# A graph network of four layers: output biases in one product, gate bias on VectorE, counting in bf16

## The chip, the cores and the metric

The kernel runs on one core of a Trainium2 chip. The metric is device time in microseconds (us) for one execution, as the median of several runs. Engines are called as in the profile: PE (TensorE; its weight loads are PEld), DVE (VectorE), ACT (ScalarE), POOL (GpSimd) and SP (SyncE, which here only issues transfers). A line of the kernel is written L2968, and a line number is always that of the kernel before.

## The reference

The input `x` has 3125 rows (nodes) of 256 numbers, and there are 50,000 edges. Four times a graph layer is added to `x`, and after each a feed-forward layer (FFN); each works on the normalised rows of `x`. The graph layers are a SAGE layer, a layer with 16 edge types (the relation layer), one attention layer, and a pair of attention layers. Two of the FFNs matter here. The one after the relation layer sends each row to one of eight experts, with a fixed capacity of rows for each:

```python
idx = jnp.argmax(probs, axis=-1)
one_hot = jax.nn.one_hot(idx, E, dtype=jnp.float32)
pos = (jnp.cumsum(one_hot, axis=0) * one_hot).sum(-1).astype(jnp.int32) - 1
kept = pos < C
```

The last one has a shared network and four experts, of which a row takes the best two, weighed by a softmax over their gates:

```python
h = jax.nn.relu(jnp.einsum('baf,efh->ebah', x, eW1) + eb1[:, None, None, :])
h = jax.nn.relu(jnp.einsum('ebah,ehg->ebag', h, eW2) + eb2[:, None, None, :])
o = jnp.einsum('ebag,ego->ebao', h, eW3) + eb3[:, None, None, :]
...
gates = jax.nn.softmax(x @ gW + gb, axis=-1)
...
return shared + gated
```

Here `shared` is a network of three layers whose last bias is `sb3`. Everything is f32.

## The kernel before

The rows stand in 25 tiles of 128 rows (the last has 53). The edges are sorted by destination and are worked through in 98 groups of four chunks of 128 edges. For each chunk POOL gathers the source rows from a table with an indirect transfer (L295). PE multiplies them with a matrix of zeros and ones, or of coefficients, into PSUM. DVE adds the result to the sums of the destination tiles: at L1423 in the attention layers, and at L2122 in the relation layer.

As soon as a destination tile has all its edges it is closed, and its share of the next step is put on a queue of generators, `self.queue`. `serve()` is called between edge groups and runs two to four steps of the front generators up to their next `yield`. So a row's routing, or a block of the last FFN, is woven into the edge work in small steps. The final order on each engine is then set by a scheduler that has its own estimate of each instruction. Each engine works its instructions in that order.

**The routing** (`switch_route`, from L2128) lies inside the relation layer, from about 1725 to 2225 us. `route(t)` normalises tile `t`, transposes it on PE (L2164), multiplies it with the gate weights (L2170), takes the softmax on DVE and ACT, and picks the best expert (`argmax`, L1666 to L1676), which gives `oh`, a 128x8 tile of zeros and ones. Two products on PE (L2186 and L2187) count the choices of the rows ahead of each row in the tile, and of the whole tile. The weights of these products are `self.tri` and `self.ones`, both 128x128. DVE adds up the counts and the place of each row (L2189 to L2205), and POOL later scatters the tile's rows into the experts' buffer (`post`, L2218). On PE the neighbours of these products are L2113, which multiplies gathered rows with spread coefficients (`terms_of`, made on DVE at L2098), and L2051, which closes a tile.

**The last FFN** (`expert_block`, from L2879) lies inside the second of the last two attention layers, from about 4400 us to the end. Its weights are loaded by `expert_weights` at about 3554 us. There are 13 blocks, one of a single tile and twelve of two. A block is normalised (L2890 to L2896) and transposed (L2904). PE makes the gates (L2915), with the gate bias as a product of one row of ones and the bias (L2916). ACT copies the gates out of PSUM (L2918). Then `expert_gates` turns them into weights on DVE and ACT (from L2859), while `layer` makes the shared and the experts' hidden layers on PE (L2923) and ACT (L2924). The gate weights are transposed on PE (L2953) and copied to `wT` by ACT (L2955). A product with `pick` spreads them (L2959) for a multiplication on DVE (L2962). For each tile of the block the output is one sum in PSUM:

```python
nc.tensor.matmul(ps[:, :D], h2[:, o], w["s3"], start=True, stop=False)                    # L2967
nc.tensor.matmul(ps[:, :D], self.ones[0:1, :], w["sb3"], start=False, stop=False)         # L2968
nc.tensor.matmul(ps[:, :D], wT[:, o], w["eb3"], start=False, stop=False)                  # L2969
...
    nc.tensor.matmul(ps[:, :D], f2[:, q, o], w["e3"][:, q, :], start=False, stop=(q == NE // 2 - 1))  # L2971
```

DVE adds it to `x` (L2974), and SP writes the tile out (L2975).

Around the last FFN, the attention layer has its own work. PE multiplies scaled rows with the edge matrices (L2514) and adds up which edges reach a row (L2398, in bf16, with the matrix `member` from a transfer). DVE and ACT scale the gathered rows `ga` (L2505 and L2510). The first two destination tiles have so many edges that they are done apart: their weights are made on DVE (L2617, L2658, L2665) and ACT (L2651, L2661) and multiplied on PE (L2669).

Of the kernel before, what the change touches and what calls it, by code (L numbers as in the profile page):

```python
# [30 lines left out]
F32 = mybir.dt.float32  # L31
I32 = mybir.dt.int32
BF16 = mybir.dt.bfloat16
F16 = mybir.dt.float16
AF = mybir.ActivationFunctionType
# [1066 lines left out]
class SortedNet(Net):  # L1102
# [1025 lines left out]
    def switch_route(self, pool):  # L2128
        nc, tc = self.nc, self.tc
        pre = "L1_ffn_"  # L2130
        NE = NE8
        wg = pool.tile([P, 2, NE], F32, name="wg")
        nc.sync.dma_start(out=wg, in_=self.ins[pre + "gate_w"].rearrange("(k p) e -> p k e", p=P))
        bg = self.load_spread(pool, pre + "gate_b", NE)
        rank = pool.tile([P, NE], F32, name="rank")
        nc.vector.tensor_scalar(rank, self.iota_row[:, :NE], -1.0, float(NE), op0=ALU.mult, op1=ALU.add)
        count = pool.tile([P, NT + 1, NE], F32, name="count")
        nc.vector.memset(count[:, 0, :], 0.0)
        tok = pool.tile([P, NT], F32, name="tok")
        nc.vector.tensor_scalar(  # L2140
            tok, self.iota_row[:, :NT], float(P), float(NE * SLOTS), op0=ALU.mult, op1=ALU.add
        )
        nc.vector.tensor_scalar(tok, tok, self.iota_col, None, op0=ALU.add)
        base = pool.tile([P, NE], F32, name="base")
        nc.vector.tensor_scalar(base, self.iota_row[:, :NE], float(SLOTS), None, op0=ALU.mult)
        self.sw_prb = self.keep.tile([P, NT], F32, name="sw_prb")
        self.sw_from = self.keep.tile([P, NT], I32, name="sw_from")

        def route(t):
            edge = self.edge  # L2150
            st = edge.tile([P, 6], F32, name="sw_st", bufs=2)
            mv = edge.tile([P, 2], F32, name="sw_mv", bufs=2)
            rs = edge.tile([P, 1], F32, name="sw_rs", bufs=2)
            nc.vector.bn_stats(out=st, in_=self.x[:, t, :])
            nc.vector.bn_aggr(out=mv, in_=st)
            nc.scalar.activation(rs, mv[:, 1:2], AF.Sqrt, bias=self.eps)
            yield
            nc.vector.reciprocal(rs, rs)
            row = edge.tile([P, D], F32, name="sw_row", bufs=6)
            nc.vector.tensor_scalar(row, self.x[:, t, :], mv[:, 0:1], rs, op0=ALU.subtract, op1=ALU.mult)  # L2160
            yield
            ps = self.bank("aux")
            for k in range(2):
                nc.tensor.transpose(ps[:, k * P : (k + 1) * P], row[:, k * P : (k + 1) * P], self.ident)  # L2164
            rT = edge.tile([P, 2, P], F32, name="sw_rT", bufs=2)
            nc.scalar.activation(rT, ps[:, : 2 * P].rearrange("p (k n) -> p k n", k=2), AF.Copy)
            yield
            ps = self.bank("aux")
            for k in range(2):
                nc.tensor.matmul(ps[:, :NE], rT[:, k, :], wg[:, k, :], start=(k == 0), stop=(k == 1))  # L2170
            g = edge.tile([P, 1, NE], F32, name="sw_g", bufs=2)
            g2 = g.rearrange("p o e -> p (o e)")
            m = edge.tile([P, 1], F32, name="sw_m", bufs=2)
            nc.vector.tensor_add(g2, ps[:, :NE], bg)
            nc.vector.tensor_reduce(m, g2, axis=AX.X, op=ALU.max)
            nc.vector.tensor_scalar(g2, g2, m, None, op0=ALU.subtract)
            nc.scalar.activation(g2, g2, AF.Exp)
            yield
            nc.vector.tensor_reduce(m, g2, axis=AX.X, op=ALU.add)
            nc.vector.reciprocal(m, m)  # L2180
            nc.vector.tensor_scalar(g2, g2, m, None, op0=ALU.mult)
            best, oh = self.argmax(edge, g, rank, 1, NE, "sw")
            oh = oh.rearrange("p o e -> p (o e)")
            yield
            ps = self.bank("aux")
            nc.tensor.matmul(ps[:, :NE], self.tri, oh, start=True, stop=True)  # L2186
            nc.tensor.matmul(ps[:, NE : 2 * NE], self.ones, oh, start=True, stop=True)  # L2187
            yield
            nc.vector.tensor_add(count[:, t + 1, :], count[:, t, :], ps[:, NE : 2 * NE])  # L2189
            place = edge.tile([P, 2, NE], F32, name="sw_place", bufs=2)  # L2190
            nc.vector.tensor_add(place[:, 0, :], ps[:, :NE], count[:, t, :])
            nc.vector.tensor_mul(place[:, 0, :], place[:, 0, :], oh)
            nc.vector.tensor_mul(place[:, 1, :], base, oh)
            spot = edge.tile([P, 4], F32, name="sw_spot", bufs=2)
            nc.vector.tensor_reduce(spot[:, 0:2], place, axis=AX.X, op=ALU.add)
            pos, eid, kept, to = (spot[:, i : i + 1] for i in range(4))
            nc.vector.tensor_scalar(kept, pos, float(CAP), None, op0=ALU.is_lt)
            nc.vector.tensor_mul(self.sw_prb[:, t : t + 1], best, kept)
            nc.vector.tensor_add(to, eid, pos)
            nc.vector.tensor_sub(to, to, tok[:, t : t + 1])  # L2200
            nc.vector.tensor_mul(to, to, kept)
            to_i = edge.tile([P, 1], I32, name="sw_to", bufs=6)
            nc.vector.tensor_add(to_i, to, tok[:, t : t + 1])
            nc.vector.tensor_scalar(pos, pos, float(CAP - 1), None, op0=ALU.min)
            nc.vector.scalar_tensor_tensor(  # L2205
                self.sw_from[:, t : t + 1], eid, CAP / SLOTS, pos, op0=ALU.mult, op1=ALU.add
            )
            self.posted.append((t, row, to_i))
            self.routes = t + 1

        return route
# [604 lines left out]
    def expert_weights(self, pool):  # L2816
# [5 lines left out]
        def load(name, shape, source, rows=None, **sizes):  # L2822
            w[name] = pool.tile(shape, F32, name="se_" + name)
            nc.sync.dma_start(out=w[name], in_=source.rearrange(rows, **sizes) if rows else source)
# [10 lines left out]
            nc.sync.dma_start(out=w["e2"][:, e, o : o + E2], in_=ins[pre + "eW2"][e])  # L2835
        load("e3", [P, NE // 2, D], ins[pre + "eW3"].rearrange("(q o) p d -> (o p) q d", o=2))
        load("gw", [P, 2, NE], ins[pre + "gW"], "(k p) e -> p k e", p=P)
        load("gb", [1, NE], ins[pre + "gb"], "(o d) -> o d", o=1)
        load("sb3", [1, D], ins[pre + "sb3"], "(o d) -> o d", o=1)
        load("eb3", [NE, D], ins[pre + "eb3"])  # L2840
        for name, n in (("sb1", 2), ("sb2", 1), ("eb1", NE), ("eb2", NE // 2)):
            a = ins[pre + name]
            rows = self.work.tile([n, P], F32, name="colrows", tag="colrows", bufs=1)
# [35 lines left out]
    def expert_block(self, w, ts):  # L2879
# [32 lines left out]
        for i in range(n):  # L2912
            o = pg[:, i * NE : (i + 1) * NE]
            for k in range(2):
                nc.tensor.matmul(o, xT[:, k, i * P : (i + 1) * P], w["gw"][:, k, :], start=(k == 0), stop=False)  # L2915
            nc.tensor.matmul(o, self.ones[0:1, :], w["gb"], start=False, stop=True)  # L2916
        g = pool.tile([P, n, NE], F32, name="se_g", tag=f"se_g{n}", bufs=1)
        nc.scalar.activation(g, pg[:, : n * NE].rearrange("p (t e) -> p t e", e=NE), AF.Copy)  # L2918

        def layer(out, weights, inputs, bias):  # L2920
            ps = self.bank("aux")
# [28 lines left out]
        yield  # L2950
        pt = self.bank("aux")
        for i in range(n):
            nc.tensor.transpose(pt[:NE, i * P : (i + 1) * P], g[:, i, :], self.ident)  # L2953
        wT = pool.tile([NE, most], F32, name="se_wT", bufs=1)[:, :N_]
        nc.scalar.activation(wT, pt[:NE, :N_], AF.Copy)  # L2955
        yield
        for q in range(NE // 2):
            ps = self.bank("aux")
            nc.tensor.matmul(  # L2959
                ps[:, :N_], w["pick"].rearrange("k e j -> k (e j)")[:, q * P : (q + 1) * P], wT, start=True, stop=True  # L2960
            )
            nc.vector.tensor_mul(f2[:, q, :], f2[:, q, :], ps[:, :N_])  # L2962
        yield
        for i, t in enumerate(ts):
            o = slice(i * P, (i + 1) * P)
            ps = self.bank("aux")
            nc.tensor.matmul(ps[:, :D], h2[:, o], w["s3"], start=True, stop=False)  # L2967
            nc.tensor.matmul(ps[:, :D], self.ones[0:1, :], w["sb3"], start=False, stop=False)  # L2968
            nc.tensor.matmul(ps[:, :D], wT[:, o], w["eb3"], start=False, stop=False)  # L2969
            for q in range(NE // 2):  # L2970
                nc.tensor.matmul(ps[:, :D], f2[:, q, o], w["e3"][:, q, :], start=False, stop=(q == NE // 2 - 1))  # L2971
            r = rows_of(t)
            xt = self.x[:r, t, :]
            nc.vector.tensor_add(xt, xt, ps[:r, :D])  # L2974
            nc.sync.dma_start(out=self.out[t * P : t * P + r, :], in_=xt)  # L2975
            yield
# [112 lines left out]
```

## Time and profile before

| | |
|---|---|
| median of 3 runs | 4983.29 us (4973.4 to 4994.1) |
| the profiled execution | 4999.19 us |
| its span in the profile | 4997.2 us |
| PE busy | 3314.8 us, 66% |
| DVE busy | 2510.3 us, 50% |
| POOL busy | 2194.3 us, 44% |
| ACT busy | 1126.5 us, 23% |

All durations in the text come from this one profiled execution. An f32 product shows as two records of PE and two weight loads, so L2968, with 25 tiles, has 50 records. "Granted clock" is the share of PE's full clock that the throttle let through in a stretch. In the views, what stands in brackets behind a row is how long the engine was idle before it and what ended that; "issue" is idle time that nothing in the profile explains.

### The profile page before, as it was taken

The page shows a single profiled execution, that of the slowest core. Times are in us where ns is not written, and L with a number is a line of the kernel's source. Part 1 is how long each engine was busy: PE and PEld are TensorE (multiplying, and loading weights), DVE is VectorE, ACT ScalarE, POOL GpSimd, SP SyncE. Part 2 cuts the span into 40 slices and gives each one's busy share as a digit, 9 for nine tenths or more (in the row PEclk, how much of TensorE's full clock was granted, in tenths as well). Part 3 has the DMA queues.
Part 4 walks back from the last instruction along what each step waited for, and adds up shares of the span by engine and source line. Part 5 has one row for each costly group of instructions (what it writes and reads, how often), then busy time and mean ns, then how long its engine had stood idle before and what let it go on. Part 6 is the DMA issues. An engine that isn't in the chain of part 4 may idle for free. (4 is left out here: it accounts for less than half of the span.)

```text
span 4997.2 us, 58241 instructions
## 1 busy us (share of the span) xinstructions
PE 3314.8 (66%) x14775; PEld 2550.4 (51%) x14775; DVE 2510.3 (50%) x8714; ACT 1126.5 (23%) x3308; POOL 2194.3 (44%) x2222
## 2 busy tenths in 40 slices
PE   3885565547985577879843565559626666278887
PEld 1554444436944566766532453449514544156665
DVE  4763253357742355651154665533536655366655
ACT  1100000012420011112221342114213522135433
POOL 3656466621046665510045556220356553554451
PEclk9997787757956777889955676669756777578878
DMA  4455366432253332223234555412445554444451
GB/s 125 128 158 145 114 181 168 112 125 76 70 174 92 90 88 81 78 69 97 66 99 122 139 150 149 140 69 72 116 128 152 158 158 129 124 125 126 135 145 53
DMA packets 423800, 590.33 MB, mean 118 GB/s; under 512 B 117955, under 2 KB 304374, under 8 KB 423076
## 3 DMA queue, kind: packets, MB, share of 16 engines
q0 software_dynamic: 106416, 287.01, 21.6%
q1 hardware_dynamic: 313838, 296.31, 19.3%
q10 hardware_dynamic: 3206, 3.20, 0.2%
q8 instruction: 125, 2.05, 0.2%
q14 instruction: 215, 1.76, 0.1%
HBM read 480.53 MB, written 105.71 MB: 117 GB/s over the span
## 5 line engine op out<-in xcount | busy, mean ns | idle before, releaser
L295 POOL DMA_INDIRECT ga<-gat_table,src_i x960 | 976.2, 1017 | 859.0 <-issue 348.9
L2514 PE MATMUL mm<-ga,oh 128*128 128x260 f32 x1920 | 685.8, 512 | 221.4 <-issue 98.7
L295 POOL DMA_INDIRECT ga<-sage_t,src_i x576 | 566.3, 983 | 369.3 <-issue 152.6
L2514 PEld LDWEIGHTS mm<-ga,oh 128*128 128x128 f32 x1920 | 461.3, 255 | 331.3 <-issue 124.6
L295 POOL DMA_INDIRECT ga<-rel_x,src_i x391 | 379.3, 970 | 249.9 <-issue 106.5
L2113 PE MATMUL mm<-terms_of,ga 128*128 128x128 f32 (+9 forms) x1564 | 306.0, 353 | 179.5 <-issue 73.3
L1447 PE MATMUL mm<-ga,oh 128*128 128x257 f32 x1152 | 327.4, 432 | 99.4 <-DVE acc L1423 36.7
L1423 DVE SCALAR_TENSOR_TENSOR acc<-mm,low,acc 128x260 f32 (+1 forms) x384 | 185.5, 483 | 375.6 <-PE mm L2514 114.2
L2113 PEld LDWEIGHTS mm<-terms_of,ga 128*128 128x128 f32 x1564 | 265.0, 242 | 212.4 <-issue 88.1
L1447 PEld LDWEIGHTS mm<-ga,oh 128*128 128x128 f32 x1152 | 240.3, 217 | 166.7 <-issue 41.1
L1934 POOL DMA_INDIRECT yt<-slot_y_d,from_i x100 | 99.2, 992 | 511.1 <-DVE terms_of L2098 225.4
L2505 DVE TENSOR_TENSOR ga<-ga,p 128x768 f32<-128x768 f32 x240 | 228.8, 955 | 74.9 <-issue 51.4
L2510 ACT ACTIVATE ga<-ga,p 128x64 f32<-128x64 f32 x960 | 259.6, 334 | 4.3 <-issue 3.6
L2122 DVE TENSOR_TENSOR terms<-terms,mm 128x256 f32 (+9 forms) x296 | 135.5, 458 | 236.7 <-remote 80.4
L1842 PEld LDWEIGHTS mm<-bT,w 128*128 128x128 f32 x1792 | 220.7, 194 | 5.6
L1842 PE MATMUL mm<-bT,w 128*128 128x128 f32 x1792 | 221.1, 277 | 0.0
L1781 POOL DMA_INDIRECT slots_d<-rows_n,slot_i x100 | 103.3, 1033 | 263.9 <-DVE oha L1676 88.2
L1860 PE MATMUL mm<-wb,hT 128*128 x896 | 211.9, 380 | 1.1 <-ACT hT L1851 1.1
L2051 PE MATMUL wide<-basis,terms 128*128 128x256 f32 x800 | 196.0, 399 | 7.1 <-issue 5.2
L2398 PE MATMUL wide<-parts,member 128*128 128x12 bf16 x960 | 54.8, 174 | 219.8 <-DMA member<-member_d 126.1
L1423 DVE SCALAR_TENSOR_TENSOR acc<-mm,high,acc 128x260 f32 (+1 forms) x384 | 184.1, 480 | 8.5 <-DVE acc L1423 3.6
L1832 ACT ACTIVATE w<-wa 128x1024 f32 x112 | 118.1, 1057 | 279.7 <-PE mm L1842 243.6
(562 smaller groups left out, 6164.4 us busy)
## 6 DMA issues: line engine op xcount, KB each, us to landing
oh<-oh_d SPq DMA_DIRECT2D x240, 256.0 KB
member<-member_d SPq DMA_DIRECT2D x240, 128.0 KB
oh_d<-oh SPq DMA_DIRECT2D x72, 256.0 KB
w<-in_L_ffn_w SPq DMA_DIRECT2D x16, 1024.0 KB
ga<-gat_table,src_i POOLq DMA_INDIRECT x960
raw<-slots_d SPq DMA_DIRECT2D x112, 128.0 KB
slot_y_d<-y SPq DMA_DIRECT2D x112, 128.0 KB
slots<-dl_d SPq DMA_DIRECT2D x80, 128.0 KB
```

The costliest lines, as they stand in the source:

```text
L295: self.nc.gpsimd.indirect_dma_start(out=out, out_offset=None, in_=table[:, :], in_offset=IndirectOffsetOnAxis(ap=idx[:, c : c + 1], axis=0),)
L1423: last = nc.vector.scalar_tensor_tensor(a, ps[:, :width], mask[:, g : g + 1], a, op0=ALU.mult, op1=ALU.add)
L1447: nc.tensor.matmul(ps[:, :width], oh, ga[:, j, :], start=(c == chunks[0]), stop=(c == chunks[-1]))
L1832: nc.scalar.activation(w.rearrange("p k h -> p (k h)"), was[:, ds(ea, W)], AF.Copy).ins
L1842: nc.tensor.matmul(ps[:, f * GS : (f + 1) * GS], w[:, k, f * P : (f + 1) * P], bT[:, k, :], start=(k == 0), stop=(k == 1),)
L1860: last = nc.tensor.matmul(ps[:, :D], hT[:, f, :], wbs[:, ds(ew + f * D, D)], start=(f == 0), stop=(f == HC - 1))
L2051: nc.tensor.matmul(ps[:, :D], a[:, k * NB + b, o : o + P], self.basis[:, k, b, :], start=(k == 0 and b == 0), stop=(k == 1 and b == NB - 1),)
L2113: nc.tensor.matmul(ps[:, k * NB * w : (k + 1) * NB * w], ga[:, j, k * P : (k + 1) * P], spread[:, j, :], start=(j == js[0]), stop=(j == js ...
L2122: nc.vector.tensor_add(a, a, ps[:, : 2 * NB * w].rearrange("p (b w) -> p b w", w=w)).ins
L2505: nc.vector.tensor_mul(body[:, :own], body[:, :own], pk[:, :own, :, None].to_broadcast([P, own, HEADS, D // HEADS]))
L2510: nc.scalar.activation(body[:, j, h, :], body[:, j, h, :], AF.Copy, scale=pk[:, j, h : h + 1])
L2514: nc.tensor.matmul(ps[:, : D + HEADS], oh[:, j, :], ga[:, j, :], start=(j == 0), stop=(j == GC - 1))
```

## The change

In the routing, the choices are cast to bf16 (`sw_one`), and so are the two weight matrices, once (`below` and `every`). A product and its weight load are now separate instructions in the program, as bf16 operands have them.

In the last FFN, the gates' tile has a fifth column that holds 1, so that its transpose `wT` has a fifth row of ones. The shared bias stands as the fifth row below the four experts' biases in one tile `b3`. One product of five rows replaces the products of one and of four rows. The gate bias is loaded spread over all 128 rows, and DVE adds it while it takes the gates out of PSUM, where ACT copied them before.

```diff
@@ switch_route
+        below = pool.tile([P, P], BF16, name="below")
+        nc.vector.tensor_copy(below, self.tri)
+        every = pool.tile([P, P], BF16, name="every")
+        nc.vector.tensor_copy(every, self.ones)
...
+            one = edge.tile([P, NE], BF16, name="sw_one", bufs=2)
+            nc.vector.tensor_copy(one, oh)
             yield
             ps = self.bank("aux")
-            nc.tensor.matmul(ps[:, :NE], self.tri, oh, start=True, stop=True)
-            nc.tensor.matmul(ps[:, NE : 2 * NE], self.ones, oh, start=True, stop=True)
+            nc.tensor.matmul(ps[:, :NE], below, one, start=True, stop=True)
+            nc.tensor.matmul(ps[:, NE : 2 * NE], every, one, start=True, stop=True)
@@ expert_weights
-        load("gb", [1, NE], ins[pre + "gb"], "(o d) -> o d", o=1)
-        load("sb3", [1, D], ins[pre + "sb3"], "(o d) -> o d", o=1)
-        load("eb3", [NE, D], ins[pre + "eb3"])
+        w["gb"] = self.load_spread(pool, pre + "gb", NE)
+        w["b3"] = pool.tile([NE + 1, D], F32, name="se_b3")
+        nc.sync.dma_start(out=w["b3"][:NE, :], in_=ins[pre + "eb3"])
+        nc.sync.dma_start(out=w["b3"][NE:, :], in_=ins[pre + "sb3"].rearrange("(o d) -> o d", o=1))
@@ expert_block
-                nc.tensor.matmul(o, xT[:, k, i * P : (i + 1) * P], w["gw"][:, k, :], start=(k == 0), stop=False)
-            nc.tensor.matmul(o, self.ones[0:1, :], w["gb"], start=False, stop=True)
-        g = pool.tile([P, n, NE], F32, name="se_g", tag=f"se_g{n}", bufs=1)
-        nc.scalar.activation(g, pg[:, : n * NE].rearrange("p (t e) -> p t e", e=NE), AF.Copy)
+                nc.tensor.matmul(o, xT[:, k, i * P : (i + 1) * P], w["gw"][:, k, :], start=(k == 0), stop=(k == 1))
+        shares = pool.tile([P, n, NE + 1], F32, name="se_g", tag=f"se_g{n}", bufs=1)
+        nc.vector.memset(shares[:, :, NE:], 1.0)
+        g = shares[:, :, :NE]
+        nc.vector.tensor_add(
+            g, pg[:, : n * NE].rearrange("p (t e) -> p t e", e=NE), w["gb"][:, None, :].to_broadcast([P, n, NE])
+        )
...
-            nc.tensor.transpose(pt[:NE, i * P : (i + 1) * P], g[:, i, :], self.ident)
-        wT = pool.tile([NE, most], F32, name="se_wT", bufs=1)[:, :N_]
-        nc.scalar.activation(wT, pt[:NE, :N_], AF.Copy)
+            nc.tensor.transpose(pt[: NE + 1, i * P : (i + 1) * P], shares[:, i, :], self.ident)
+        wT = pool.tile([NE + 1, most], F32, name="se_wT", bufs=1)[:, :N_]
+        nc.scalar.activation(wT, pt[: NE + 1, :N_], AF.Copy)
...
-            nc.tensor.matmul(ps[:, :D], self.ones[0:1, :], w["sb3"], start=False, stop=False)
-            nc.tensor.matmul(ps[:, :D], wT[:, o], w["eb3"], start=False, stop=False)
+            nc.tensor.matmul(ps[:, :D], wT[:, o], w["b3"], start=False, stop=False)
```

The product with `pick` (L2959) reads the first four rows of `wT` as before.

More of the change, by code (lines that the diff above doesn't have):

```diff
@@ L2959, in expert_block @@
             nc.tensor.matmul(
-                ps[:, :N_], w["pick"].rearrange("k e j -> k (e j)")[:, q * P : (q + 1) * P], wT, start=True, stop=True
+                ps[:, :N_], w["pick"].rearrange("k e j -> k (e j)")[:, q * P : (q + 1) * P], wT[:NE, :], start=True, stop=True
             )
```

## The prediction, made before the changed kernel ran

> **What bounds the kernel now.** The change touches two stages, so I first read busy time and granted clock in stretches, then the chain of waits in the last one, then single rows.
>
> ```profile
> 1725.00:2225.00 500.00, 402.42 (x1942) 347.57 (x1940) 293.98 (x1205) 88.70 (x104) 250.24 (x254) 0.81 0.25 73
> 1850.00:1950.00 100.00, 77.13 (x387) 67.80 (x386) 55.96 (x227) 17.03 (x18) 57.58 (x58) 0.75 0.28 81
> 2050.00:2150.00 100.00, 86.95 (x411) 74.27 (x410) 65.61 (x261) 17.75 (x21) 53.19 (x54) 0.88 0.27 78
> 4400.00:4900.00 500.00, 416.60 (x1836) 308.29 (x1836) 315.82 (x1204) 215.55 (x733) 238.66 (x236) 0.82 0.48 134
> 4900.00:4997.00 97.00, 77.22 (x298) 58.90 (x297) 47.54 (x185) 32.18 (x108) 0.00 (x0) 0.80 0.09 28
> ```
>
> After the length come PE, weight loads, DVE, ACT and POOL, then the clock. The first row is the routing stage, the last two are the last attention layer with the last FFN inside it. In both PE is busy some 80% and nothing else is over 63%: PE sets the pace, with gaps.
>
> The chain of waits from 4350 us to the end, by line:
>
> ```profile
> by line: PE mm L2514 25.3%; PE aux L2923 15.3%; issue 8.8%; PE aux L2971 5.4%; PE aux L2968 3.1%; PE aux L2967 2.8%; PE hub L2669 2.4%; PE aux L2969 2.3%; DMA member<-member_d 2.1%; DVE ga L2505 1.9%; PE aux L2915 1.9%; DVE acc L1423 1.9%;
> ```
>
> L2968, the shared bias product that the change removes, holds 3.1% of 648 us there, 20 us. Its 50 rows are busy 22.6 us in that stretch, so 88% of it lies on the chain. For the routing stage the trace gives no chain.
>
> **The output biases.** The timeline's weight loads of one 128-row output tile, at full clock:
>
> ```profile
> 4918.07 0.41 PEld L2967 LDWEIGHTS aux<-se_s,se_h 128*128 128x128 f32 x2
> 4918.81 0.29 PEld L2968 LDWEIGHTS aux<-se_sb,ones 1*128 1x128 f32 x2 [0.33 <-issue]
> 4919.13 0.40 PEld L2969 LDWEIGHTS aux<-se_eb,se_wT 4*128 4x128 f32 x2
> 4919.87 0.73 PEld L2971 LDWEIGHTS aux<-se_e,se_f 128*128 128x128 f32 x4 [0.33 <-issue]
> ```
>
> Each f32 product is two records. L2968 goes and L2969 takes five rows in place of four. The products stand at 4918.81 (L2968) and 4919.35 (L2969), so one removed product frees 0.54 us; a fifth row adds no column, and the products of one row and of four rows both stream at the same step. At the clock of 0.82 that is 0.66 us, over 25 tiles 16.5 us.
>
> The 0.33 us ahead of L2968 and of L2971 is a stop between products of 128 rows and of few rows. Five rows leave both stops, so I count no gain from them.
>
> **The gate bias.**
>
> ```profile
> 4399.50 0.52 PEld L2915 LDWEIGHTS aux<-se_gw,se_xT 128*128 128x128 f32 x4 [0.49 <-ACT se_xT L2905]
> 4400.04 0.29 PEld L2916 LDWEIGHTS aux<-se_gb,ones 1*128 1x128 f32 x2
> 4400.35 0.52 PEld L2915 LDWEIGHTS aux<-se_gw,se_xT 128*128 128x128 f32 x4
> ```
>
> L2916 goes: from its load to the next tile's first is 0.31 us, at 0.82 0.38 us, over 25 tiles 9.5 us. L2916 follows L2915 by 0.54 us, four loads at 0.135, so no stop shows here.
>
> The Trainium skill (TensorEngine Tiling (Array Packing), section Key Properties) says that changing the tiling mode drains the engine. By that each gate bias would also cost two stops, and their removal would make the sum some 20 us larger. The rows ahead of L2971 agree with it, those of L2916 don't, and the rows decide.
>
> PE is thus freed of 26 us; with 88% on the chain that is -23 us. DVE gets 13 memsets (at most 0.11 us, the 128x64 row of L2419) and 13 adds from PSUM (0.17 us, the routing's own L2174): 3.6 us in a stretch where it is idle 37%. ACT loses 13 copies of 0.18 us and the hop from ACT to DVE goes. I count this as zero, with the wait itself among the rivals. The transposes and their ACT copy take five rows instead of four at no cost that a row would show. The three loads at L2824 stay three on SP's queue in the same place, at 3554 us, over 800 us before use; some one-hot loads move one to six SP issues, 0.3 us each, and are read ahead.
>
> **The counting products.**
>
> ```profile
> 2012.76 0.41 PEld L2186 LDWEIGHTS aux<-ohsw,tri 128*128 128x128 f32 x2
> 2013.08 0.30 PEld L2187 LDWEIGHTS aux<-ohsw,ones 128*128 128x128 f32 x2
> 2013.31 0.57 PEld L2113 LDWEIGHTS mm<-terms_of,ga 128*128 128x128 f32 x4
> 4524.37 0.42 PEld L2398 LDWEIGHTS <-member 128*128 128x128 bf16 x11 [0.28 <-issue]
> 4524.71 0.32 PEld L2514 LDWEIGHTS mm<-ga,oh 128*128 128x128 f32 x2
> ```
>
> In f32 both take 0.55 us a tile. The nearest bf16 rows are L2398's, the same load and 12 columns: 11 in 0.34 us, 0.03 us each, with up to 0.28 us of idle ahead of a batch. So the new pair costs 0.06 to 0.34 us; I take 0.15, near the low end, since most of that idle may be the wait for the batch's own data. That frees 0.40 us at full clock, 0.49 us at 0.81, over 25 tiles 12 us (bounds 6.5 and 15). It isn't all on the path: POOL waits for PE's L2113 76 us in this stage, but PE waits for "issue" 46 us, so the pace goes round PE, DVE and POOL. I take six tenths: -7 us.
>
> Added are 25 casts on DVE (at most 0.17 us each, the row of L1676) ahead of the products. PE waited for the choices nine times (8.4 us "issue", 8.1 us DVE); nine hops of 0.2 us are +2 us. Two 128x128 copies at the start (0.23 us, L96) lie beside PE's work on the relation rows. In the built order the pair stands mostly one or a few large products later than before, and eight scatters on POOL stand a few gathers later; both let work pass that used to wait, and I count them as zero, 5 us either way.
>
> **The sum.** -23 - 7 + 2 = -28 us. From the profiled 4999.19 us (span 4997.2, 2 us around it) that gives 4971; that execution is 16 us above the median of 4983.29, so on the median's scale 4955.3 us, -0.56%.
>
> **The rivals.**
>
> *Covered.* PE ends its part earlier and waits for something else. For it: PE is idle 83 of 500 us in the last layer, part of it for DVE's scaling L2505 and the DMA of member masks. Against it: those waits follow from PE's own pace, as POOL's gathers hang on buffers that PE frees. A third of the gain would be left: -10 us, 4973.
>
> *The clock.* The granted clock goes with PE's share: 77 of 100 us busy at 0.75, 87 at 0.88, 0.013 a point. In the routing stage 12 us less of 500 are 2.4 points, 0.03 of clock, 4% of 400 us: +16 us, so 4971. Against it: a slower clock also lengthens the busy time, and in the last layer more work doesn't go with more clock (43 of 50 us busy at 0.73 from 4600 us, 40 at 0.86 from 4550). The Trainium skill (TensorE: Matmul & The Clock Gate, section HAM oscillation) has gaps of over 3.4 us halve the clock; removed products make few of those.
>
> *Stops at the gate.* If L2916 hides two stops of 0.33 us a tile, another 20 us at 0.82 go: 4935. No row shows it.
>
> *Slower: DVE waits for the gate.*
>
> ```profile
> ACT se_g L2918 <- PE aux L2916: 13.4, 6, 3.7
> DVE se_m L2859 <- ACT se_g L2918: 10.9, 5, 4.1
> ```
>
> (Waits from 4400 us on: us, times, longest.) ACT, idle for most of this stage, waited for the gate product; now DVE does, in order, and behind the add stand the hub weights L2665 and the sums L1423, which free PE's banks, and L2505, which feeds PE. In the built order L2665 or L1423 stands a few places behind the add in most of the 13 blocks. For 13 blocks all of ACT's idle ahead of L2918, 31 us, is 2.4 us a block; added whole to my sum that makes +3. It decides from 4 us a block (52 - 28 = +24 us, about 5008). Against it: DVE already waits here one step later, and the gate product now comes 0.8 us earlier a block.
>
> That the change doesn't do what it says I leave out: the built order has 50 products fewer and the bf16 loads in place.
>
> **How the numbers follow.** Forecast 0.58 (-18 to -42 us, by the bounds above), stops at the gate 0.06, covered 0.17, clock 0.05, slower 0.14. Half a per cent is 25 us, about what a measurement of this kernel can tell from no change. Eight tenths of the forecast lie beyond it: faster 0.46 + 0.06 = 0.52; same 0.12 + 0.17 + 0.05 = 0.34; slower 0.14. The range reaches from 4925, past the stops, to 4996, past the covered cases and into small losses; it leaves out most of the slower case.
>
> **What would show it.** Right: the last layer is some 23 us shorter, PE's busy time in it is about 25 us less, and the chain's share for the one product of five rows stays near 2.3%. In the routing stage the loads of the pair take 0.1 us in place of 0.55. Wrong: the new add waits over 4 us a block with L2665 and L1423 late behind it; idle of 0.3 us on both sides of the bf16 pair; or the routing stage as long as before with PE idler.

## The result, and the profile after

| first comparison, 12 runs each | before | after |
|---|---|---|
| median | 4989.76 us | 4951.69 us |
| lowest to highest | 4969.01 to 5013.15 | 4926.56 to 4980.96 |
| the profiled execution (its span) | 4999.19 (4997.2) | 4937.48 (4935.4) |

The changed kernel takes 0.9927 [0.9906, 0.9948] of the time of the kernel before: 38 us less by the medians. The forecast was -28. The same two kernels were compared twice more (`e5_all` and `e10_all_again` below) and gave 0.9975 [0.9952, 0.9997] and 0.9955 [0.9934, 0.9976]. By these ratios the gains are 36, 13 and 20 us, 23 on average; by the medians they are 38, 16 and 28. So the forecast is of the right size, and the first comparison was a favourable one; the 13 us of the second lie nearer to the rival *covered* (-10) than to the forecast.

In the changed kernel the lines have moved: the counting pair is L2192 and L2193, the cast L2189, the gate product L2922, the new add L2926, the output sum L2977 (shared), L2978 (five rows) and L2980 (experts), the attention product L2520.

Stretches of the profile of after, with the columns of the first view of before. The first row is the routing stage in the same 500 us as before. The second is the last layer from the first gate product to the end.

```profile
1725.00:2225.00 500.00, 386.60 (x1881) 328.42 (x1881) 295.39 (x1223) 87.75 (x102) 248.15 (x251) 0.82 0.26 74
4358.90:4935.40 576.50, 462.40 (x2035) 342.62 (x2035) 364.24 (x1413) 246.56 (x830) 242.39 (x236) 0.83 0.43 121
```

The same last stretch of before, from its first gate product at 4399.50:

```profile
4399.50:4997.20 597.70, 494.32 (x2135) 367.70 (x2135) 363.36 (x1389) 248.23 (x843) 239.11 (x236) 0.82 0.42 116
```

It is 21.2 us shorter (23 were forecast), PE is busy 31.9 us less in it (25 were forecast), and 100 records of PE are gone, 50 for each product removed. PE's idle time (length less busy) grows from 103 to 114 us: a third of what PE saves returns as waiting. Busy time times granted clock estimates PE's work at full clock: 405 us before, 384 after, so 21 less. The clock has two digits, so each product is good to 2 or 3 us. The prediction's own 25 tiles of 0.54 and 0.31 us give 21.3. One pair of executions shows little of the length: `e5_all` below runs the code of after and takes 593.3 us in this stretch.

The routing stage, from the first counting load to the last, goes from 500.2 to 493.7 us. Of the 62 us between the two profiles, these two stretches give 28. Of the other 34, 29.5 lie between the two stretches and 4.6 ahead of them, where the change touches only the loads at 3554 us and two copies at 1500 us. The 12 runs of the kernel before range over 44 us, so I take the 34 for scatter between single executions; that isn't shown.

One output tile of after in the timeline, weight loads at full clock:

```profile
4866.77 0.41 PEld L2977 LDWEIGHTS aux<-se_s,se_h 128*128 128x128 f32 x2
4867.51 0.29 PEld L2978 LDWEIGHTS aux<-se_b,se_wT 5*128 5x128 f32 x2 [0.33 <-issue]
4868.13 0.73 PEld L2980 LDWEIGHTS aux<-se_e,se_f 128*128 128x128 f32 x4 [0.33 <-issue]
4868.89 0.41 PEld L2977 LDWEIGHTS aux<-se_s,se_h 128*128 128x128 f32 x2
```

Before, the tile shown in the prediction was followed by the next tile's first load:

```profile
4920.62 0.41 PEld L2967 LDWEIGHTS aux<-se_s,se_h 128*128 128x128 f32 x2
```

From one tile's first load to the next tile's first it is now 2.12 us, against 2.55 before (4918.07 to 4920.62). The product freed 0.43 us, not 0.54. The two products of few rows took 1.06 us together, up to the load of L2971; the one takes 0.62 up to that of L2980. So the distance of 0.54 between the two starts wasn't what one of them adds. Both stops of 0.33 us stay, as forecast.

The gate of after, one block of two tiles:

```profile
4358.94 0.97 PEld L2922 LDWEIGHTS aux<-se_gw,se_xT 128*128 128x128 f32 x8 [0.49 <-ACT se_xT L2912]
4359.83 0.73 PEld L2933 LDWEIGHTS aux<-se_xT,se_s 128*128 128x128 f32 x4
```

The second tile's gate of before ended with these lines:

```profile
4400.88 0.29 PEld L2916 LDWEIGHTS aux<-se_gb,ones 1*128 1x128 f32 x2
4401.19 0.73 PEld L2923 LDWEIGHTS aux<-se_xT,se_s 128*128 128x128 f32 x4
```

From the gate's first load to the next product's it is 0.89 us, against 1.69 before (4399.50 to 4401.19): 0.40 us a tile is freed, where 0.31 was forecast. The other 0.09 us were in the loads of L2915: the four of a tile took 0.54 us before and take 0.445 now.

A counting pair of after in the timeline, then what PE and POOL waited for in the routing stage (us, times, longest):

```profile
2010.80 0.10 PEld L2192 LDWEIGHTS <-below 128*128 128x128 bf16 x1
2011.02 0.10 PEld L2193 LDWEIGHTS <-every 128*128 128x128 bf16 x1
2011.05 0.30 PEld L2051 LDWEIGHTS wide<-basis,terms 128*128 128x128 f32 x2
```

```profile
POOL ga L295 <- PE mm L2113: 95.5, 37, 8.9
PEld L2192 <- DVE sw_one L2189: 9.9, 4, 4.6
PE aux L2192 <- DVE sw_one L2189: 8.9, 3, 4.5
PEld L2193 <- issue: 3.2, 4, 1.2
```

A load takes 0.10 us, where the prediction read 0.03 from the rows of L2398, and the pair holds PE's loads for 0.25 us, not 0.15: it frees 0.30 us a tile in place of 0.40. (Over all 25 pairs, at the granted clocks, the median of this distance goes from 0.71 to 0.30 us.) The two middle rows count the same waits twice, once on the queue of the loads and once on that of the products, as the longest one shows in the timeline of each:

```profile
2209.37 0.10 PEld L2192 LDWEIGHTS <-below 128*128 128x128 bf16 x1 [4.61 <-DVE sw_one L2189]
2209.38 0.19 PE L2192 MATMUL aux<-sw_one,below 128*128 128x8 bf16 x1 [4.52 <-DVE sw_one L2189]
```

So PE's loads wait 9.9 us in 4 places for the cast choices; before, the loads of L2186 waited 9.1 us in 6. The cast has added little to those waits. POOL waits longer for PE's L2113 than before (95.5 us against 76.3).

In the chain of waits of the last layer, by line, from 4310 us on:

```profile
by line: PE mm L2520 23.4%; PE aux L2933 15.5%; issue 9.2%; another core or an unknown queue 6.5%; PE aux L2980 4.6%; DVE acc L1423 2.7%; PE aux L2978 2.7%; DMA member<-member_d 2.6%; PE aux L2922 2.5%; PE aux L2977 2.4%; PE hub L2675 2.2%; 
```

The five-row product holds 2.7% of 626 us, where 2.3% was forecast. The 3.1% of L2968 are gone. An unknown queue, which was not among the first lines before, now holds 6.5%, but half of that stands ahead of the first gate product (three waits of 19.9 us from 4321 us on). Inside the last layer it holds five waits of 19.6 us among the chain's longest pieces, against three of 9.5 us before. The masks' transfer holds 2.6% in place of 2.1%.

### The profile page after: what moved, and what is told of

It is laid out like the page before. It is cut to its first block, busy times and chain, and to the rows that moved or that the text cites. A ratio compares the mean times of both kernels' runs of the same rounds, so it can differ in the third digit from the quotient of the medians.

```text
span 4935.4 us, 57961 instructions
## 1 busy us (share of the span) xinstructions
PE 3259.6 (66%) x14625; PEld 2501.9 (51%) x14625; DVE 2514.7 (51%) x8767; ACT 1123.1 (23%) x3295; POOL 2198.4 (45%) x2222
## 5 line engine op out<-in xcount | busy, mean ns | idle before, releaser
L2520 PE MATMUL mm<-ga,oh 128*128 128x260 f32 x1920 | 681.4, 510 | 221.5 <-issue 75.4
L2520 PEld LDWEIGHTS mm<-ga,oh 128*128 128x128 f32 x1920 | 459.4, 254 | 331.8 <-issue 100.8
L2113 PE MATMUL mm<-terms_of,ga 128*128 128x128 f32 (+9 forms) x1564 | 308.2, 354 | 182.4 <-issue 88.4
L2113 PEld LDWEIGHTS mm<-terms_of,ga 128*128 128x128 f32 x1564 | 266.7, 243 | 216.1 <-issue 100.4
L1447 PE MATMUL mm<-ga,oh 128*128 128x257 f32 x1152 | 325.8, 429 | 71.0 <-issue 23.3
```

The source lines that it names most:

```text
L1447: nc.tensor.matmul(ps[:, :width], oh, ga[:, j, :], start=(c == chunks[0]), stop=(c == chunks[-1]))
L2113: nc.tensor.matmul(ps[:, k * NB * w : (k + 1) * NB * w], ga[:, j, k * P : (k + 1) * P], spread[:, j, :], start=(j == js[0]), stop=(j == js ...
L2520: nc.tensor.matmul(ps[:, : D + HEADS], oh[:, j, :], ga[:, j, :], start=(j == 0), stop=(j == GC - 1))
```

## The experiments

There are three series; in each the kernels and the kernel before ran on one chip. The chips differ: the kernel before takes 4990 us on the chip of the first comparison (which chip that was isn't known), 5016 on that of the second series, 4511 and 4509 on those of the first and the third. So each ratio is to the kernel before on the same chip. "Last layer" is from the first gate product to the end, in one profile.

**The parts, each alone.** The first series. `e1_counts` is the kernel before with the part of the diff under `switch_route` alone, `e2_ffn` has the other two parts alone, and the other two halve that again:

```diff
e3_five: e2_ffn with the gate of before
-        w["gb"] = self.load_spread(pool, pre + "gb", NE)
+        load("gb", [1, NE], ins[pre + "gb"], "(o d) -> o d", o=1)
-                nc.tensor.matmul(o, ..., w["gw"][:, k, :], start=(k == 0), stop=(k == 1))
+                nc.tensor.matmul(o, ..., w["gw"][:, k, :], start=(k == 0), stop=False)
+            nc.tensor.matmul(o, self.ones[0:1, :], w["gb"], start=False, stop=True)
...
-        nc.vector.tensor_add(g, pg[...], w["gb"][...])
+        nc.scalar.activation(g, pg[...], AF.Copy)
e4_gate: the kernel before, with the gate bias spread and added on DVE
-        load("gb", [1, NE], ins[pre + "gb"], "(o d) -> o d", o=1)
+        w["gb"] = self.load_spread(pool, pre + "gb", NE)
...
-            nc.tensor.matmul(o, self.ones[0:1, :], w["gb"], start=False, stop=True)
...
-        nc.scalar.activation(g, pg[...], AF.Copy)
+        nc.vector.tensor_add(g, pg[...], w["gb"][...])
```

> The kernel before with the counting products in bf16 alone. In the trace, from the first to the last counting product took 500.2 us before and 493.7 us with the whole change. Theory (each part gains the PE time that it frees, in its own stage): this stretch 490 to 497 us, the time 4 to 10 us below the kernel before, everything from the attention layers on as before. Rival (the counting also speeds up or shifts what follows, and accounts for most of the 38 us between the medians): the time 20 us or more below. Rival (the cast ahead of the products costs what the products gain): stretch 500 us or more, time not below.

> The kernel before with the last FFN's part alone: five rows in one product, gate bias on VectorE. From the first gate product to the end took 597.7 us before and 576.5 us with the whole change. Theory: 573 to 582 us, the time 17 to 26 us below the kernel before. Rival (the gain is larger than the PE time freed because the order of the last layer fell better): 570 us or less. Rival (a gain outside of the changed stages comes with the whole change): this part alone gives much less than 38 us and the counting alone doesn't make up the rest.

> The kernel before with only the output biases in one product of five rows; the gate bias stays a product on PE and ACT copies the gates. An output tile took 2.55 us of PE at full clock before and 2.12 after, 0.43 us or 13 us over 25 tiles at a clock of 0.82. Theory: from the first gate product to the end 12 to 15 us less than 597.7, so 583 to 586 us, time 10 to 16 us below. Rival (the bias products were covered by other waits): 592 us or more. Rival (the move of the gate to DVE costs, and this part carries all of the gain): 578 us or less.

> The kernel before with only the gate bias added on VectorE; the output biases stay two products. Theory: 9.5 us of PE freed, most of it on the path, so from the first gate product to the end 587 to 591 us, time 6 to 10 us below. Rival (DVE waits for the gate in order and gives the gain back): 597 us or more, with long idle of DVE ahead of the add. Rival (each gate bias also cost two stops of PE, 0.33 us each): 575 us or less.

| | ratio | routing stage | last layer | PE busy | clock | busy x clock |
|---|---|---|---|---|---|---|
| e1_counts | 0.9983 [0.9953, 1.0013] | 463.9 us | 545.9 us | 466.4 us | 0.85 | 396 us |
| e2_ffn | 0.995 [0.9925, 0.9975] | 472.7 | 517.3 | 438.2 | 0.87 | 381 |
| e3_five | 1.0013 [0.9991, 1.0036] | 474.6 | 547.1 | 462.8 | 0.83 | 384 |
| e4_gate | 0.9966 [0.9942, 0.999] | 472.1 | 530.8 | 454.2 | 0.86 | 391 |

By whole runs the FFN's part and the gate bias alone are faster than the kernel before; the counts alone and the five rows alone can't be told from it. For the five rows 10 to 16 us were expected.

In the profiles, the routing stage is 9 us shorter with the counts in bf16 than in the other three (mean 473). The last layer of `e1_counts` is that of before, and the FFN's part takes 28.6 us off it; the gate bias alone takes 15, and the five rows alone take nothing. These lengths hold to a dozen us only: `e9_null` below runs the code of `e1_counts` in this stretch and takes 558.0 us. The stretch of the last layer of `e1_counts`, then of `e3_five`:

```profile
3962.60:4508.50 545.90, 466.41 (x2135) 353.44 (x2135) 363.10 (x1389) 248.44 (x843) 245.71 (x243) 0.85 0.47 129
```

```profile
3976.90:4524.00 547.10, 462.81 (x2085) 350.01 (x2085) 362.70 (x1400) 248.74 (x843) 243.61 (x242) 0.83 0.47 129
```

PE has 50 records less, and its work at full clock falls by 12 us. But the clock stands at 0.83 in place of 0.85, and PE's busy time falls by 3.6 us only. At 0.85 the 384 us of work would take 452 us, 11 less than were measured. In this pair a lower clock took the saving back. That the lower clock belongs to the five rows isn't shown: against `e9_null`, at a clock of 0.82, `e3_five` is 11 us shorter. For it speaks that over its 12 runs `e3_five` has a mean clock of 0.7903, the kernel before 0.7927, the other three 0.7947 to 0.7951.

**The products doubled and left out.** The second series, with the full change again (`e5_all`). `e6_double` adds to the kernel before one more one-row product for each output tile, with weights of zero. `e7_no_shared_bias` leaves the shared bias out of the result, and `e8_no_gate_bias` the gate bias; ACT still copies the gates.

```diff
e6_double
             nc.tensor.matmul(ps[:, :D], self.ones[0:1, :], w["sb3"], start=False, stop=False)
+            none = w["e2"].rearrange("p e j -> p (e j)")[0:1, 64 : 64 + P]
+            nc.tensor.matmul(ps[:, :D], none, w["sb3"], start=False, stop=False)
e7_no_shared_bias
-            nc.tensor.matmul(ps[:, :D], self.ones[0:1, :], w["sb3"], start=False, stop=False)
e8_no_gate_bias
-                nc.tensor.matmul(o, ..., w["gw"][:, k, :], start=(k == 0), stop=False)
-            nc.tensor.matmul(o, self.ones[0:1, :], w["gb"], start=False, stop=True)
+                nc.tensor.matmul(o, ..., w["gw"][:, k, :], start=(k == 0), stop=(k == 1))
```

> The changed kernel once more, beside the parts. The kernel before took 4511 us in the first four comparisons, some 480 us less than when the change was first measured, on other silicon. Theory (the gain is PE time, most of it in the last layer): routing stretch 460 to 467 us, from the first gate product to the end 514 to 521 us, the time 25 to 35 us below the kernel before. Rival (much of the first 38 us belonged to that chip, or to chance): 10 to 20 us below.

> The kernel before with one more product of one row a tile (25 more): the shared bias once more, weighed with zeros. It prices one such product from the other side. Theory (a bias product is PE time on the path at 0.54 us at full clock): from the first gate product to the end 10 to 16 us longer than 545.9. Rival (such a product is covered, as the five rows alone suggested with no gain): within 4 us. Rival (which way a small edit goes here is set by how the order falls and by the clock that is granted with it): a change of more than 16 us or a shorter stretch, with a clock other than 0.81 in it.

> The kernel before without the shared output bias: its product of one row is left out and nothing takes its place, so PE gets what the five rows alone give it, with the gates' tile and its transpose untouched. Theory (the PE time is on the path and the five rows alone lost it elsewhere, in their own order): 10 to 16 us less than 545.9 from the first gate product to the end. Rival (covered): within 4 us of it. Rival (clock): PE records per us as in e3_five with the clock lower, near 0.80, and no gain.

> The kernel before without the gate bias: its product is left out, and ACT still copies the gates. It parts the two things that moving the gate bias did: PE's product gone, and the copy moved from ACT to DVE. Theory (PE time alone): from the first gate product to the end 7 to 10 us less than 545.9. Rival (the move off ACT's queue is what gained): within 3 us of it. Rival (both stops of PE at the gate go too): 14 us less or more, as with the move.

| | ratio | last layer | PE busy | PE idle | clock | busy x clock |
|---|---|---|---|---|---|---|
| e5_all | 0.9975 [0.9952, 0.9997] | 593.3 us | 473.6 us | 119.7 us | 0.81 | 384 us |
| e6_double | 1.0038 [1.0017, 1.0059] | 593.5 | 501.6 | 91.9 | 0.82 | 411 |
| e7_no_shared_bias | 0.9987 [0.9962, 1.0013] | 596.9 | 483.4 | 113.5 | 0.81 | 392 |
| e8_no_gate_bias | 0.9958 [0.9933, 0.9983] | 594.5 | 477.1 | 117.4 | 0.82 | 391 |

The stretch of the last layer of `e5_all`, then of `e6_double`:

```profile
4396.00:4989.30 593.30, 473.62 (x2035) 349.40 (x2035) 364.06 (x1414) 247.06 (x830) 241.66 (x236) 0.81 0.42 117
```

```profile
4404.80:4998.30 593.50, 501.56 (x2185) 377.01 (x2185) 364.67 (x1389) 247.03 (x843) 243.16 (x236) 0.82 0.43 117
```

PE has 150 records and 28 us of busy time less in the one than in the other, and the stretch is equally long. In these two executions all of PE's saving went into PE's idle time. That is the rival *covered* at its purest. It is no rule, since by twelve runs the two kernels are 0.63% apart, some 30 us. The gate bias left out gains about as much as the add in its place (0.9958, and 0.9966 in `e4_gate`). ACT still copies the gates in `e8_no_gate_bias`, so the gain comes from the product that PE no longer makes, and the move from ACT to DVE isn't needed for it. The shared bias left out gains 0.13%, which isn't told apart from nothing; doubled, it costs 0.38%.

The full change gains 13 us here, the 10 to 20 us of its rival and not the 25 to 35 expected. Its routing stage takes 497.1 us, 3.9 less than the mean of the other three (501.0). The lengths expected of the last layer (from 545.9 us) were those of a faster chip and can't be held against this series, and it has no profile of the kernel before.

**No change, the full change, and two further steps.** The third series. `e9_null` is the kernel before, compared with itself, and `e10_all_again` the full change. `e11_pair` is the full change with the five-row products of both tiles of a block first and back to back, so that a block has half as many stops. In `e12_pair_nocast`, which has the order of the full change and not the pair, the comparison that picks the expert writes its zeros and ones in bf16 itself, without the cast.

```diff
e11_pair
+        sums = []
+        for i in range(n):
+            sums.append(self.bank("aux"))
+            nc.tensor.matmul(sums[i][:, :D], wT[:, i * P : (i + 1) * P], w["b3"], start=True, stop=False)
...
-            ps = self.bank("aux")
-            nc.tensor.matmul(ps[:, :D], h2[:, o], w["s3"], start=True, stop=False)
-            nc.tensor.matmul(ps[:, :D], wT[:, o], w["b3"], start=False, stop=False)
+            ps = sums[i]
+            nc.tensor.matmul(ps[:, :D], h2[:, o], w["s3"], start=False, stop=False)
e12_pair_nocast
-            best, oh = self.argmax(edge, g, rank, 1, NE, "sw")
-            oh = oh.rearrange("p o e -> p (o e)")
-            one = edge.tile([P, NE], BF16, name="sw_one", bufs=2)
-            nc.vector.tensor_copy(one, oh)
+            one = edge.tile([P, 1, NE], BF16, name="sw_one", bufs=2)
+            best, oh = self.argmax(edge, g, rank, 1, NE, "sw", out=one)
+            one = oh = oh.rearrange("p o e -> p (o e)")
```

> The kernel before against itself, to see what a comparison and a single profile can tell. Expected: a ratio of 1 within 0.3%. The stretches of one profile vary too: the last layer from the first gate product to the end took 576.5 us in one execution of the changed kernel and 593.3 us in another on other silicon, so I expect it within 12 us of 597.7 here if the times are near 5000 us, and the routing stretch, which varied by 1 us between kernels that leave it alone, within 2 us of 500 (or of 473 if the times are near 4510 us).

> The changed kernel a third time, to settle between 36 us (first comparison) and 12 to 17 us (e5_all). Theory (about 28 us on average, and chips differ in how much of the freed PE time is covered): 12 to 36 us below the kernel before; routing stretch 4 to 9 us shorter than that of e9_null, the last layer from the first gate product to the end 8 to 25 us shorter. Rival (nearly all of the freed time is covered where transfers are slow): below 8 us.

> The changed kernel, with the five-row products of both tiles of a block issued back to back and first, so that PE changes between products of 128 and of few rows twice a block and not twice a tile. The stop of 0.33 us stands ahead of each such change: 24 stops fewer, 0.33 us at 0.82, 10 us of PE. Theory (the stop belongs to the change of row count): stops ahead of these products halve, 3 to 10 us less than e10_all_again. Rival (the stop comes with each few-row product, or is covered): no change within 5 us. Rival (both PSUM banks are now held for the whole output of a block, so the next user waits): slower than e10_all_again.

> The changed kernel without the cast in the routing (the output order of e11 isn't in it): the last comparison of the expert choice writes bf16 itself, and the counting products and the two multiplications on DVE read that tile. 25 casts of 0.17 us go from DVE and one step from the way of the choices to PE. Theory (PE waited for the cast about as long as before for the choices, 19 us in all): routing stretch 2 to 5 us shorter than e10_all_again, time too small to tell. Rival (the products are off the path): stretch within 1 us.

| | ratio | routing stage | last layer | PE busy | clock | busy x clock |
|---|---|---|---|---|---|---|
| e9_null | 1.0016 [0.9992, 1.0039] | 471.4 us | 558.0 us | 486.8 us | 0.82 | 399 us |
| e10_all_again | 0.9955 [0.9934, 0.9976] | 463.1 | 518.3 | 437.1 | 0.87 | 380 |
| e11_pair | 0.9954 [0.9933, 0.9974] | 462.0 | 522.0 | 440.8 | 0.86 | 379 |
| e12_pair_nocast | 0.9954 [0.9932, 0.9976] | 461.4 | 527.1 | 445.2 | 0.86 | 383 |

The stretch of the last layer of `e9_null`, then of `e10_all_again`:

```profile
3963.50:4521.50 558.00, 486.81 (x2135) 366.87 (x2135) 363.33 (x1389) 248.64 (x843) 247.02 (x242) 0.82 0.45 126
```

```profile
3945.00:4463.30 518.30, 437.05 (x2035) 329.15 (x2035) 362.87 (x1413) 246.69 (x830) 251.15 (x243) 0.87 0.48 136
```

Here the stretch is 40 us shorter, where 8 to 25 were expected, and the clock goes up as PE's work goes down by 19 us at full clock. PE's busy time falls by 50 us: the work's 19 us are 23 at 0.82, and the other 27 go with the clock; PE's idle time grows by 10. `e9_null` and `e1_counts` run the same code in this stretch, and differ by 12 us at clocks of 0.82 and 0.85.

The two further steps show no gain over `e10_all_again`; the intervals are some 9 us wide on either side, so a gain of a few us isn't ruled out. In `e11_pair` the stops are halved, as one block in the timeline shows:

```profile
4410.08 0.72 PEld L2977 LDWEIGHTS aux<-se_b,se_wT 5*128 5x128 f32 x4 [0.34 <-DVE se_f L2972]
4411.14 0.30 PEld L2981 LDWEIGHTS aux<-se_s,se_h 128*128 128x128 f32 x2 [0.33 <-issue]
4411.46 0.84 PEld L2983 LDWEIGHTS aux<-se_e,se_f 128*128 128x128 f32 x4
4412.32 0.41 PEld L2981 LDWEIGHTS aux<-se_s,se_h 128*128 128x128 f32 x2
4412.76 0.84 PEld L2983 LDWEIGHTS aux<-se_e,se_f 128*128 128x128 f32 x4
```

Two changes of the number of rows stand in a block in place of four, at 0.33 us each. In the whole stage the idle time put down to "issue" ahead of the loads of the output sum goes from 18.4 us (46 times) in `e10_all_again` to 8.9 (21 times). A part of it is only put down to DVE now, as in the first line above: with every cause counted, the idle time there goes from 21.0 to 15.2 us. The Trainium skill (TensorEngine Tiling (Array Packing), section Key Properties) says that a change of the tiling mode drains the engine, and these rows agree. The 5.8 us less do not show in the time of 12 runs. Without the cast PE's loads wait 8.3 us for the choices in the routing stage, in place of 9.9, so the cast wasn't most of what they waited for. That stage is 1.7 us shorter than in `e10_all_again`, where 2 to 5 were expected; `e11_pair`, which has the cast, is 1.1 shorter.

**What the scatter goes with.** On the chip of each series, the runs of one kernel with a higher mean granted clock are the shorter ones: the correlation of time with clock is -0.66 to -0.88 in the 35 runs of the kernel before. Within kernels the time falls by 29.0, 28.1 and 29.2 us for each 0.01 of mean clock on the three chips. Before's runs in the second series go from 0.755 (5038.53 us) to 0.770 (4987.59 us). So the kernels can be compared as if at equal clock (mean times, moved by that slope to the clock of before; the error is one standard error of the kernel's own runs, and that of the kernel before, 1.0 to 1.8 us, comes on top):

| at equal clock, us to before | |
|---|---|
| counting alone: e1_counts | -0.5 ± 3.1 |
| last FFN alone: e2_ffn | -15.7 ± 2.5 |
| five rows alone: e3_five | +0.2 ± 1.9 |
| gate bias alone: e4_gate | -9.0 ± 1.7 |
| full change: e5_all, e10_all_again | -11.3 ± 2.8, -23.3 ± 1.5 |
| shared bias product doubled, left out: e6, e7 | +7.9 ± 4.1, -7.3 ± 3.5 |
| gate bias product left out: e8 | -14.2 ± 3.5 |
| full change with the pair, without the cast: e11, e12 | -18.2 ± 2.7, -17.5 ± 1.5 |
| no change: e9_null | -1.2 ± 2.4 |

The table is a reading of the runs and no experiment: nothing here set the clock, and less work on PE may itself move it. It does make doubling and leaving out agree: a one-row product with 256 columns for each tile is worth 7 to 8 us at the end, with an error of 4. And it leaves the full change at 11 us in the second series and 23 in the third, so by this reading the chips differ in how much of the saving comes out.

## Why the prediction was right, and where it wasn't

**The sum was about right.** -28 us was forecast; -38, -16 and -28 were measured by the medians, -36, -13 and -20 by the ratios. That the sum came so near owes something to chance: its terms were off both ways, and the first two comparisons lie further apart (0.0048) than the interval of either reaches (0.0023).

**PE sets the pace, with gaps.** Right as far as it goes. In the last layer PE's work fell by 15 to 21 us at full clock with the whole FFN part in (405 to 384 us in the first comparison, 396 to 381 in the first series, 399 to 380 in the third), where the loads' distances in the timeline give 25 tiles of 0.43 and 0.40, 21 us. The mean of the three executions with the code of before is 400 us, that of the four with both FFN parts (after, `e2_ffn`, `e5_all`, `e10_all_again`) 382, so 18. How much of it reaches the end is less steady than the 88% read from the chain: it went from nothing (`e5_all` against `e6_double`) to more than all (`e10_all_again` against `e9_null`), as idle time and clock moved.

**The output biases** were too large a term: 0.54 us a tile was taken, 0.43 measured, so 13 us at 0.82 in place of 16.5. And of that less reached the end than the 88%: 0 to 7 us by `e3_five`, `e7_no_shared_bias` and `e2_ffn` less `e4_gate`, all in the table at equal clock. So it isn't shown that the five rows alone make the kernel faster.

**The gate bias** was too small: 0.40 us a tile against 0.31, 12 us at 0.82, and 9 to 14 us reach the end in the table at equal clock. The prediction read the 0.54 us ahead of L2916 as four equal loads; 0.09 of them went with the product. Why more of it gets through than of the output bias isn't shown. The two errors nearly cancel: 25 us were freed where 26 were forecast.

**The counting** freed 0.30 us a tile and not 0.40, since the pair costs 0.25 us. The nearest bf16 rows, eleven loads in a row, weren't a price for a lone pair. The stage is 6.5 us shorter in the first two profiles and 9, 3.9 and 8.3 in the three series, where -5 was forecast for it. But by whole runs the counts alone give 0.9983 [0.9953, 1.0013], at equal clock nothing, so whether those 4 to 9 us reach the end stays open. The +2 us for the cast came from nine waits, which were six: the 8.4 us of "issue" stand on the queue of the loads and most of the 8.1 us of DVE are the same time on that of the products. Their 9.1 us became 9.9, and 8.3 without the cast, so the term was some 1 us. (The 46 us of "issue" on PE are 42 in the stretch of the first view; nothing hangs on it.)

**The rivals.** *Slower: DVE waits for the gate* fell. Before, DVE waited 18.6 us at L2859 for the gate (10.9 for ACT and 7.7 put down to "issue"). The new add waits 11.8 us for PE:

```profile
DVE se_g L2926 <- PE aux L2922: 11.8, 8, 2.7
```

That is 0.9 us for each of 13 blocks, and the longest is 2.7; it would have had to be 4 on average. *Stops at the gate* fell too: a tile frees 0.40 us, and two hidden stops would have made it 0.97. *Covered* is a part of the truth: PE's idle time grows by 11 us in the first comparison, and by all that was saved in one pair of profiles, and the second comparison's 13 us are near its price. *The clock* was priced in the wrong way: as a loss that follows from a smaller share of PE. It took back 11 us in `e3_five` against `e1_counts`, but in `e2_ffn`, `e10_all_again` and the two others of that series the clock was higher with less work. The Trainium skill (TensorE: Matmul & The Clock Gate, section HAM oscillation) ties a lower clock to idle gaps of PE of over some 3.4 us. In the last layer `e9_null` has 3 such gaps between products and a clock of 0.82, `e10_all_again` 4 and 0.87; `e1_counts` has 3 and 0.85, `e3_five` 4 and 0.83. So neither their number nor the sum of idle time (71 us in `e9_null`, 81 in `e10_all_again`) explains the clock, and what sets it stays open.

**Zero for stalls moved.** The memsets and adds on DVE show in no wait: in the last layer no wait of DVE grew by more than 7 us, and those that grew most (6 us each, L2381 and L2441 of after) are waits for PE. In the routing stage POOL's wait for L2113 grew by 19 us while the stage got shorter; whether the moved scatters have a part in that isn't shown.

## What to carry to other kernels

Price a removed product by the distance between the loads of its neighbours, per tile and at full clock, and allow 0.1 us a product for what the neighbours themselves lose or gain (0.54 was taken for 0.43 here, 0.31 for 0.40). Check it afterwards by PE's busy time times its granted clock: that sum stays within 9 us for one code (396 to 405 in three executions) where the stage's length moves by fifty between chips. Where PE is busy 80% of a stage, a third to all of what it saves may come out (here 13, 20 and 36 us of 25 + 9), and single executions say little on that share. A gain of half a per cent here, some 24 us, is twice the scatter of single runs (12 to 14 us, one standard deviation in the 35 runs of the kernel before), so one comparison doesn't settle its size, and a part of the change alone can read as nothing.

## What the runs showed of the hardware

The same program takes 4510 us on two chips, with a mean clock of 0.793, and 5016 on a third, with 0.763 (4990 in the first comparison, whose chip isn't known). The clock doesn't make up the whole: in the last layer PE is idle for 71 us of 558 (`e9_null`) and for 103 of 598 (before, profiled at 0.763), so where the program is slower PE also waits longer.

Between the 35 runs of the kernel before on one chip the mean granted clock moves by 0.003 (one standard deviation), and within kernels the time goes with it by 28 to 29 us for 0.01.

A change between products of 128 rows and of 1, 4 or 5 rows with 256 columns shows 0.33 us of idle time ahead of the load. The gate's product of one row and 4 columns (L2916 at 4400.04 us) shows none.
